# Cross attention with a second attention beside it: two small softmax operations on Pool, the exponential behind the transposed copies, and two products of the keys exchanged

## The chip, the cores and the metric

The kernel runs on one core of one Trainium2 chip. The metric is the device time of one execution in microseconds (us); the time before is 937.95 us, the median of 3 runs (937.41 to 938.43). A core has five engines that run side by side, each with its own queue of instructions: TensorE (PE) for matmuls, VectorE (DVE), ScalarE (ACT) and GpSimd (Pool) for everything elementwise, and SyncE (SP), which here only issues DMAs. An instruction waits at the head of its engine's queue until the instructions it depends on have signalled, and all behind it wait as well.

## What is computed

For 16 batch elements there are 100 query rows of 640 features (x) and 722 context rows of 384 features. The last 4 context rows are tokens of their own. All is float32.

```
query, keyt, valt = x @ Wq, enc @ Wk, enc @ Wv        # enc: 718 context rows
hs = mha(query, keyt, valt)                           # 8 heads of 80
ca_q1 = einsum('btc,th->bch', ca, Wq_ca)[:, indices]  # ca: 4 tokens, 100 picked rows
ca_hs1 = mha(ca_q1, x, x)
ca_q2, ca_k2, ca_v2 = ca_hs1 @ Wq, ca @ Wk_ca, ca @ Wv_ca
out = (hs + mha(ca_q2, ca_k2, ca_v2)) @ Wout + b_out + x
```

The first attention (hs) is large. The other two, called the second attention here, are small; the change is in the softmax of the last of them, which has 100 rows, 8 heads and 4 tokens, so 100 x 32 numbers.

## The kernel before, in words

The batch loop (L1218) makes 16 passes, b = 0 to 15. A pass interleaves three things: the first attention of element b, the keys and values that are needed next (values of b, keys of b+1), and the second attention of b+1 in its first half and of b in its second half. From L1217 on the order is written by hand: every engine's queue holds its instructions in the order in which the program text issues them, and no scheduler moves them.

PE's order in a pass of the usual kind (b = 1 to 14) is: scores of element b (L622, three groups), the product z of the second attention (L810) and y for the next element (L748), then 15 products for the values (L442, class `Values`, called vv) and 15 for the keys (L473, class `Keys`, kk) in turns, then the last chunk of the keys (L567), in some passes an output projection (L1033), in odd passes the queries of the next two elements (L543), and the attention times the values (L1433).

The values and the keys are formed by a scheme with 15 products of sums of input blocks in place of 18 plain ones. Products are accumulated in five PSUM banks, A to E, by the order in `V_PLAN` and `K_PLAN` (L104, L122). Each entry names the bank, the product's form and the place (u, g) of the result to which the bank, as it stands after this product, is added. `Blocks.go` (L404) issues the product, then the drain: a copy on ACT (L415) if the place is new, else an add on DVE (L413). As a bank goes on being accumulated, the next product in the same bank must wait until the bank has been read:

```
for out, left in self.places(at, to):
    if to in self.begun:
        self.moved = nc.vector.tensor_tensor(out, left, out, ALU.add)
    else:
        self.moved = nc.scalar.copy(out, left)
```

The keys' last six entries are, before: B (place 0,1), C (0,1), A (0,1), C (2,1), B (0,0), A (1,1). The first of these is a copy on ACT, the C after it an add on DVE. In a usual pass the end of the product stage issues, by L1346 to L1358: two products vv and one kk; `subtract(0)` and `exponential(0)`; vv; `subtract(1)`; vv; two kk; `exponential(1)`; vv; two kk; then vv and kk in turn, twice. After that come the loads for b+2, `subtract(2)`, `exponential(2)` and the last chunk of the keys. `subtract(i)` (L1240) is a DVE instruction on 120 x 1600 numbers that takes the maximum of the first attention's scores from them in place; both inputs are in SBUF. `exponential(i)` (L1248) is ACT's.

The maximum itself is found by `Maximum` (L658) in steps: transposes and reductions on DVE, then a copy that spreads it (on ACT, L696), then a transpose on DVE (`over`, L704).

The second attention is in the class `Second`. `scores1` (L776) is Pool's: four multiplies (L783) and three adds (L790) of 100 x 800 numbers, for element b+1; the first one waits for the DVE instruction `seen`, the end of the maximum's third part. `scores2` (L837), for element b, forms on DVE the sum s2 (L840), its maximum mx2 (L847), the difference e2 (L849), and on ACT the exponential (L852). `softmax3` (L855) forms on DVE the sum (L858), its reciprocal (L859) and the product p2 (L861). `values2` (L866) is Pool's again: four multiplies by p2 (L875) and three adds (L882), 100 x 640.

The class `Last` ends an element. `turn` and `place` (L932, L937) transpose its result and lay it down with 12 to 20 or so small copies on ACT (L948). `load` (L904) fetches rows of x and adds the bias on Pool (L915, the xn adds). In the passes b = 3, 6, 8, 11 and 13, the pair passes, the projection of two row blocks is done as one (`sums` L1006, `project_pair` L1016): there Pool makes the sum of two blocks (L1014), then, among PE's products, differences (L1050, L1053) and a form of the weights (L1054) that PE multiplies with. After that Pool makes the second attention's keys (L720) and the sums for the next keys and values (L508).

In a usual pass Pool's queue thus holds, before: scores1 of b+1, the xn adds (pair passes), values2 of b, the sums and the projection's operands (pair passes), the vb loads (L832), L720, L508.

Of the kernel before, what the change touches and what calls it, by code (L numbers as in the profile page):

```python
# [9 lines left out]
AF = mybir.ActivationFunctionType  # L10
# [6 lines left out]
CAD, T = 384, 4  # L17
# [28 lines left out]
SCALE = float(D) ** -0.5  # L46
# [72 lines left out]
    ("A", 5, (1, 1)),  # L119
]  # L120

K_PLAN = [V_PLAN[k] for k in (0, 1, 2, 3, 4, 6, 5, 7, 9, 11, 8, 12, 10, 13, 14)]  # L122


A_RAW = {(0, 0): 0, (0, 1): 1, (0, 2): 2, (1, 1): 3, (1, 2): 4, (2, 0): 5, (2, 1): 6}
# [10 lines left out]
def kernel(  # L136
# [18 lines left out]
    nc = tc.nc  # L155
# [220 lines left out]
    def first_values(i, enc, engines, halves=(0, 1), get=psum):  # L376

        u, j = KC[i]
        for g in halves:
            engine = engines[g]  # L380
            v_ps = get(f"v_ps_0_{i}_{g}")
            for c in range(CC):
                nc.tensor.matmul(
                    v_ps[:KN, : H // 2],
                    a_raw(enc, u, c)[:, j * KN : (j + 1) * KN],
                    wv_sb[:, 2 * c + g],
                    start=(c == 0),
                    stop=(c == CC - 1),
                )
            engine(  # L390
                block(i, g)[:, :, :D],
                v_ps[:KN, : H // 2].rearrange("p (h d) -> p h d", d=D),
            )
# [333 lines left out]
    class Second:  # L727
# [45 lines left out]
                ],  # L773
            )

        def scores1(self, behind=None):  # L776
            b, g = self.b, self.g
            e = e1[:S].rearrange("p (h s) -> p h s", h=NH)
            for t in range(T):
                to = e if t == 0 else product_tile(f"e1_{b}_{t}")[:S].rearrange(  # L780
                    "p (h s) -> p h s", h=NH
                )
                first = nc.gpsimd.tensor_tensor(  # L783
                    to,
                    self.ca[:, t, :].unsqueeze(1).to_broadcast([S, NH, S]),
                    g[:, :, t].unsqueeze(2).to_broadcast([S, NH, S]),
                    ALU.mult,
                )
                if t:
                    nc.gpsimd.tensor_tensor(e, e, to, ALU.add)  # L790
                elif behind:
                    wait_for(first, behind)
# [41 lines left out]
            )  # L834
            return vb

        def scores2(self):  # L837
            b, z = self.b, self.z
            s2 = small.tile([S, NH, T], F32, tag="s2", name=f"s2_{b}")
            nc.vector.tensor_reduce(  # L840
                s2.rearrange("p h t -> p (h t)"),
                z.rearrange("p h k -> p k h"),
                AX.X,
                ALU.add,
            )
            mx = small.tile([S, NH], F32, tag="mx2", name=f"mx2_{b}")
            nc.vector.tensor_reduce(mx, s2, AX.X, ALU.max)  # L847
            e = small.tile([S, NH, T], F32, tag="e2", name=f"e2_{b}")
            nc.vector.tensor_tensor(  # L849
                e, s2, mx.unsqueeze(2).to_broadcast([S, NH, T]), ALU.subtract  # L850
            )
            nc.scalar.activation(e, e, AF.Exp, scale=SCALE)  # L852
            self.e = e

        def softmax3(self):  # L855
            b, e = self.b, self.e
            sm = small.tile([S, NH], F32, tag="sm2", name=f"sm2_{b}")
            nc.vector.tensor_reduce(sm, e, AX.X, ALU.add)  # L858
            nc.vector.reciprocal(sm, sm)  # L859
            p2 = small.tile([S, NH, T], F32, tag="p2", name=f"p2_{b}")  # L860
            nc.vector.tensor_tensor(  # L861
                p2, e, sm.unsqueeze(2).to_broadcast([S, NH, T]), ALU.mult
            )
            self.p2 = p2
# [280 lines left out]
    second = Second(0, xT, ca_0)  # L1145
# [72 lines left out]
    for b in range(B):  # L1218
        p = b // 2
        e_in, now = enc, second  # L1220
        enc, second = enc_next, second_next
# [56 lines left out]
        if b == 0:  # L1278
            second.scores1()
            m_next = load_m(b + 2)  # L1280
            kk.go(3)
            top.go(3)
            first_values(3, e_in, (act, act), get=bank)
            top.go(1)
            kk.go(2)
            now.scores2()
            first_values(0, e_in, (act, act), (0,), bank)
            top.go()
            kk.go(3)
            first_values(0, e_in, (act, act), (1,), bank)  # L1290
            now.softmax3()
            kk.go(2)
            subtract(0)
            exponential(0)
            kk.go(2)
            subtract(1)
            kk.go(3)
            exponential(1)
            second_next, enc_next = loads()
            less = subtract(2)  # L1300
            exponential(2)
            last_keys(b + 1, enc)
            enc_next = load_rest(b + 2, enc_next)
            keys(m_next)
            now.values2(less)
            enc_sums(enc_next)
            second.softmax1(4)
        elif b + 1 < B:
            vv = Values(b, e_in)

            def both(n):
                vv.go(n)
                kk.go(n)

            forms = [wout_sb[:, 2 * i : 2 * i + 2, k * (H // 2) : (k + 1) * (H // 2)]
                     for i in range(2) for k in range(2)]
            if b == 2:
                for o, left, right in (
                    (forms[1], forms[1], forms[0]),
                    (wout2[:, 0], forms[3], forms[1]),  # L1320
                    (wout2[:, 1], forms[2], wout2[:, 0]),
                ):
                    nc.gpsimd.tensor_tensor(o, left, right, ALU.subtract)
            elif last.b - 1 in PAIRS:
                nc.gpsimd.tensor_tensor(wout2[:, 0], wout2[:, 0], forms[0], ALU.add)
            second.scores1(seen)
            if b == 1:
                now.load()
            last.load()
            top.go(3)  # L1330
            both(3)
            now.scores2()
            top.go(1)
            if b > 1:
                last.place()
            both(2)
            both(2)
            top.go()
            both(1)
            now.softmax3()  # L1340
            if b == 1:
                nc.gpsimd.tensor_tensor(last.hs[:S], last.hs[:S], last.hs2, ALU.add)
            now.values2()
            if last.b in PAIRS:
                last.sums()
            vv.go(2)  # L1346
            kk.go(1)
            subtract(0)
            exponential(0)
            vv.go(1)  # L1350
            subtract(1)
            vv.go(1)
            kk.go(2)
            exponential(1)
            vv.go(1)
            kk.go(2)
            both(1)
            both(1)  # L1358
            if b == 1:
                for f in list(wv_there):  # L1360
                    nc.scalar.copy(wv_sb[:, W_AT[f]], wv_there.pop(f))
            second.load()
            if b == 1:
                nc.gpsimd.dma_start(out=bias, in_=bout[0].partition_broadcast(P))
            second_next, enc_next = loads()
            if b + 2 < B:
                m_next = load_m(b + 2)
            subtract(2)
            exponential(2)
            last_keys(b + 1, enc)  # L1370
            if b + 2 < B:
                enc_next = load_rest(b + 2, enc_next)
            if b == 1:
                last.transpose()
            if last.b in PAIRS:
                second.softmax1(3)
                last.project_pair()
                if last.b == max(PAIRS):
                    nc.sync.dma_start(
                        out=forms[1],  # L1380
                        in_=wout[: 2 * P, H // 2 :].rearrange("(c p) n -> p c n", p=P),
                    )
            second.softmax1()
        else:
            room = enc_tile("spare").rearrange("p f k -> p (f k)")
            spare.extend(room[:, i * H : (i + 1) * H] for i in range(2))
            last.transpose()
            vv = Values(b, e_in)
            last.load()
            mine.load()  # L1390
            top.go(3)
            vv.go(3)
            last.project_few(len(OC) - 2)
            now.scores2()
            top.go(1)
            vv.go(2)
            top.go()
            vv.go(3)
            now.softmax3()
            now.values2()  # L1400
            vv.go(2)
            subtract(0)
            exponential(0)
            vv.go(5)
            for i in (1, 2):
                subtract(i)
                exponential(i)
            last.project()
# [105 lines left out]
```

## Time and profile before

| what | before |
|---|---|
| median of 3 runs | 937.95 us (937.41 to 938.43) |
| the profiled execution | 936.77 us, span 935.1 us |
| granted TensorE clock | 1.0 of full speed |
| L849 (e2, DVE) | 16 instructions, 900 ns median, 191 to 1249 ns |
| L861 (p2, DVE) | 16 instructions, 193 ns median, 191 to 1573 ns |
| L852 (exponential, ACT) | 16 instructions of 229 ns; ACT idle 27.2 us before them |
| L1240 (subtract, DVE) | 48 instructions, mean 2257 ns, 1810 to 2893 ns |
| L875 (multiply, Pool) | 64 instructions, mean 1882 ns, shortest 1264 ns |
| L720 (Pool, 128 x 64 and 128 x 96) | 70 instructions, median 294 ns |
| Pool idle before L783 for DVE's most | 116.7 us in 9 waits |

The span goes from the first to the last instruction; the rest of an execution's time lies around it. A row of the timeline gives the start in us from the span's start, the time, the engine, the source line and what is written from what; "xN" means N instructions in the row, and a bracket says how long the engine stood idle before it and who released it. PE has two rows: matmuls (PE) and the weight loads (PEld) that run ahead of them. The ends of matmuls are modelled, so their starts are the better measure.

### The profile page before, as it was taken

What the parts mean: (1) busy time and instruction counts of PE and PEld (TensorE: products, weight loads), DVE (VectorE), ACT (ScalarE), POOL (GpSimd) and SP (SyncE); (2) the same over time, 40 slices, a digit from 0 to 9 for tenths busy, and PEclk for the clock granted to TensorE, in tenths of its full rate; (3) what the DMA queues carried; (4) which work ended last, traced back from release to release, by engine and by line L of the source; (5) the groups of instructions that cost most, each with busy time, mean ns of one, the idle gap of its engine ahead of it and who ended that gap; (6) DMA issues with size and microseconds to landing.
All of it is one profiled execution on the core that took longest, in us unless ns stands there. A gap on an engine that the chain in (4) does not pass through costs nothing.

```text
span 935.1 us, 25893 instructions
## 1 busy us (share of the span) xinstructions
PE 926.5 (99%) x11130; PEld 786.6 (84%) x11130; DVE 699.4 (75%) x1111; ACT 434.6 (46%) x836; POOL 674.8 (72%) x615
## 2 busy tenths in 40 slices
PE   9999999999999999999999999999999999999998
PEld 6998989797797979888798787988879888797866
DVE  3859794989739796795957869589883898838884
ACT  2235443736337363562726536264651737417341
POOL 5657998788937877496884968658895588946723
PEclk9999999999999999999999999999999999999999
DMA  8732022040300304031030400205030050310201
GB/s 258 260 96 70 24 78 64 12 143 2 107 26 23 104 11 122 2 103 53 26 106 3 124 31 30 74 2 153 3 102 31 2 153 2 102 45 2 81 19 40
DMA packets 49673, 62.82 MB, mean 67 GB/s; under 512 B 14072, under 2 KB 38200, under 8 KB 49560
## 3 DMA queue, kind: packets, MB, share of 16 engines
q1 hardware_dynamic: 45512, 51.49, 18.3%
q0 software_dynamic: 3024, 8.53, 3.0%
q8 instruction: 87, 1.43, 0.6%
q10 hardware_dynamic: 1024, 1.15, 0.4%
q14 instruction: 26, 0.21, 0.1%
HBM read 55.59 MB, written 5.57 MB: 65 GB/s over the span
## 4 chain that ended last, share of the span: by engine, by line
PE 86%; DVE 11%; issue 1%; DMA 1%; ACT 1%; POOL 0%; DVEq 0%
PE a_ps L1433 12%; PE s_ps L622 12%; PE v_psA L442 8%; PE kT_ps L567 8%; PE q_ps L543 7%; PE v_psB L442 7%; PE k_psA L473 6%; PE o_ps L1033 5%; PE k_psB L473 5%; PE v_psC L442 3%; DVE st L1240 3%; DVE vs L413 2%; PE k_psC L473 2%; DVE kT L413 2%; DVE most L1252 2%; PE y_ps L748 2%
## 5 line engine op out<-in xcount | busy, mean ns | idle before, releaser
L783 POOL TENSOR_TENSOR e<-ca,g 100x800 f32<-100x800 f32 x64 | 99.5, 1564 | 130.6 <-DVE most L1252 116.7
L875 POOL TENSOR_TENSOR hs<-vb,p 100x640 f32<-100x640 f32 x64 | 119.8, 1882 | 49.7 <-DVE p L861 24.1
L508 POOL TENSOR_TENSOR enc<-enc 128x240 f32<-128x240 f32 x135 | 106.2, 796 | 20.4 <-DMA enc<-in_enct 13.3
L1433 PEld LDWEIGHTS a_ps<-vs,st 120*36 120x36 f32 (+3 forms) x3072 | 109.2, 125 | 4.9 <-issue 4.8
L1433 PE MATMUL a_ps<-vs,st 120*36 120x81 f32 (+3 forms) x3072 | 112.0, 233 | 0.0
L442 PE MATMUL v_psA<-wv_sb,enc 128*120 128x320 f32 x352 | 109.6, 434 | 0.0
L1240 DVE TENSOR_TENSOR st<-st,over 120x1600 f32<-120x1600 f32 x48 | 108.3, 2257 | 0.0
L882 POOL TENSOR_TENSOR hs<-hs,hs 100x640 f32<-100x640 f32 x48 | 99.1, 2065 | 3.8
L622 PE MATMUL s_ps<-qp,kT 32*120 32x100 f32 x3072 | 98.3, 263 | 0.0
L622 PEld LDWEIGHTS s_ps<-qp,kT 32*120 32x120 f32 x3072 | 95.5, 179 | 1.7 <-issue 0.2
L639 ACT COPY st<-s_ps 120x800 f32<-120x800 f32 x64 | 49.7, 829 | 100.6 <-PE s_ps L622 100.6
L790 POOL TENSOR_TENSOR e<-e,e 100x800 f32<-100x800 f32 x48 | 92.3, 1922 | 3.8
L442 PE MATMUL v_psB<-wv_sb,enc 128*120 128x320 f32 x296 | 91.8, 433 | 0.0
L1248 ACT ACTIVATE st<-st 120x1600 f32<-120x1600 f32 x48 | 73.8, 1538 | 32.6 <-DVE st L1240 32.4
L473 PE MATMUL k_psA<-enc,wk_sb 128*128 128x240 f32 x360 | 87.6, 366 | 0.0
L1252 DVE TENSOR_TENSOR most<-most,st 120x800 f32<-120x800 f32 x64 | 68.4, 1068 | 22.4 <-ACT st L633 21.3
L473 PEld LDWEIGHTS k_psA<-enc,wk_sb 128*128 128x128 f32 x360 | 68.3, 190 | 16.7
L442 PEld LDWEIGHTS v_psA<-wv_sb,enc 128*120 128x120 f32 x352 | 63.2, 183 | 22.6 <-issue 0.5
L473 PE MATMUL k_psB<-enc,wk_sb 128*128 128x240 f32 x300 | 73.1, 366 | 0.1
L442 PEld LDWEIGHTS v_psB<-wv_sb,enc 128*120 128x120 f32 x296 | 54.1, 183 | 21.9 <-DVE vs L413 0.4
L1445 DVE RECIPROCAL rs<-a_ps 100x4 f32<-100x4 f32 x32 | 5.8, 181 | 85.6 <-PE a_ps L1433 85.6
L948 ACT COPY hsT<-turned_hs 32x160 f32<-32x160 f32 (+7 forms) x244 | 67.7, 278 | 3.0
(167 smaller groups left out, 1852.8 us busy)
## 6 DMA issues: line engine op xcount, KB each, us to landing
vb<-va_d POOLq DMA_DIRECT2D x32, 250.0 KB, 3.6
vb<-va_d SPq DMA_DIRECT2D x32, 250.0 KB
enc<-in_enct SPq DMA_DIRECT2D x30, 240.0 KB
enc<-in_enct SPq DMA_DIRECT2D x15, 360.0 KB
xT<-in_xt SPq DMA_DIRECT2D x8, 500.0 KB
rest<-in_enct SPq DMA_DIRECT2D x31, 120.0 KB
xn<-in_x SPq DMA_DIRECT2D x11, 320.0 KB
out<-xn SPq DMA_DIRECT2D x11, 320.0 KB
```

What stands on the lines that cost most here:

```text
L442: nc.tensor.matmul(at[0][j][:KN, : H // 2], a_form(self.enc, f)[:, j * KN : (j + 1) * KN], wv_there.get(f, wv_sb[:, W_AT[f]]), start=first ...
L473: nc.tensor.matmul(at[:, i * KT : (i + 1) * KT], wk_sb[:, W_AT[f], i], a_form(self.enc, f), start=(first and i == 0), stop=last, skip_grou ...
L508: nc.gpsimd.tensor_tensor(out, left, right, op)
L567: nc.tensor.matmul(bank[:, i * KT : (i + 1) * KT], weights[c], a_raw(enc, u, c), start=(i == 0 and c == 0), stop=(c == CC - 1), skip_group ...
L622: nc.tensor.matmul(s_ps[r][:n, 256 * a + lo : 256 * a + hi], kT[rows, c, u, j * KN : (j + 1) * KN], rhs, start=(a == 0 and c == 0), stop=( ...
L783: first = nc.gpsimd.tensor_tensor(to, self.ca[:, t, :].unsqueeze(1).to_broadcast([S, NH, S]), g[:, :, t].unsqueeze(2).to_broadcast([S, NH, ...
L790: nc.gpsimd.tensor_tensor(e, e, to, ALU.add)
L875: first = nc.gpsimd.tensor_tensor(to, self.vb[t][:S].rearrange("p (h d) -> p h d", h=NH), p2[:, :, t].unsqueeze(2).to_broadcast([S, NH, D] ...
L882: nc.gpsimd.tensor_tensor(sums, sums, to, ALU.add)
L1240: return nc.vector.tensor_tensor(st[i], st[i], top.over[:KN].unsqueeze(1).to_broadcast([KN, 2, ROWS]), ALU.subtract,)
L1252: most_now = nc.vector.tensor_tensor(most[:KN], most[:KN], st[i][:, u], ALU.max)
L1433: nc.tensor.matmul(a_v[lo:hi, h % 4], st[i // 2][: KEYS[i], i % 2, h * S + lo : h * S + hi], block(i, h // 4)[: KEYS[i], h % 4], start=(i ...
```

## The change

In `K_PLAN` the entries C (2,1) and B (0,0) near the end change places, so that the keys' last five products are C, A, B, C, A.

`scores1` can be issued in parts. In the usual passes (b = 1 to 14) Pool gets three of the four multiplies with their two adds, then the difference e2 of `scores2` (with an engine as its argument, here Pool), then the fourth multiply with its add. The exponential is a method of its own and is issued behind the spread copies and behind `place`. In the last pass e2 is on Pool as well, its exponential stays where it was; in the first pass e2 stays on DVE. The product p2 of `softmax3` goes to Pool in all passes, directly ahead of the multiplies of `values2` in the usual ones, and ahead of L720 in pass 0. The numbers computed are the same.

```diff
-K_PLAN = [V_PLAN[k] for k in (0, 1, 2, 3, 4, 6, 5, 7, 9, 11, 8, 12, 10, 13, 14)]
+K_PLAN = [V_PLAN[k] for k in (0, 1, 2, 3, 4, 6, 5, 7, 9, 11, 8, 12, 13, 10, 14)]
...
-        def scores1(self, behind=None):
+        def scores1(self, behind=None, tokens=range(T)):
...
-            for t in range(T):
+            for t in tokens:
...
-        def scores2(self):
+        def scores2(self, engine=nc.vector):
...
-            nc.vector.tensor_tensor(
+            engine.tensor_tensor(
                 e, s2, mx.unsqueeze(2).to_broadcast([S, NH, T]), ALU.subtract
             )
-            nc.scalar.activation(e, e, AF.Exp, scale=SCALE)
             self.e = e
+
+        def exponentials2(self):
+            nc.scalar.activation(self.e, self.e, AF.Exp, scale=SCALE)
...
-            nc.vector.tensor_tensor(
+            nc.gpsimd.tensor_tensor(
                 p2, e, sm.unsqueeze(2).to_broadcast([S, NH, T]), ALU.mult
             )
...
-            second.scores1(seen)
+            second.scores1(seen, range(T - 1))
+            top.go(3)
+            both(3)
+            now.scores2(nc.gpsimd)
+            second.scores1(None, range(T - 1, T))
             if b == 1:
                 now.load()
             last.load()
-            top.go(3)
-            both(3)
-            now.scores2()
             top.go(1)
             if b > 1:
                 last.place()
+            now.exponentials2()
             both(2)
...
-            now.scores2()
+            now.scores2(nc.gpsimd)
+            now.exponentials2()
```

More of the change, by code (lines that the diff above doesn't have):

```diff
@@ L1393 @@
             last.project_few(len(OC) - 2)
-            now.scores2()
+            now.scores2(nc.gpsimd)
+            now.exponentials2()
             top.go(1)
```

## The prediction

> **What bounds the kernel now.** I read the page first, then who waits for whom, then the chain of waits, then the timeline of single passes. A pass is one round of the batch loop, numbered by b.
>
> ```profile
> PE 926.5 (99%) x11130; PEld 786.6 (84%) x11130; DVE 699.4 (75%) x1111; ACT 434.6 (46%) x836; POOL 674.8 (72%) x615
> ```
>
> TensorE (PE) is busy for 926.5 of 935.1 us, so work taken off another engine pays only where PE stands still for it. The list of waits has one PE wait that returns in every pass:
>
> ```profile
> PEld k_psC L473 <- DVE kT L413: 7.8, 15, 1.0
> PE k_psC L473 <- DVE kT L413: 1.9, 4, 0.6
> ```
>
> The keys' second C product waits until VectorE (DVE) has added the first one out of the same bank. Part of the weight load's wait is covered by the matmul before it, so I take the loss from PE's starts. From the start of the eleventh keys' A product to the product after C there should be two keys' products of 0.81 us, 1.62 us. The time above that is, for passes 0 to 14: 0.59, 0.17, 0.33, 0.91, 0.33, 0.33, 0.17, 0.33, 0.15, 0.33, 0.33, 0.75, 0.34, 0.75, 0.36. The sum is 6.17 us. Pass 7 shows the cause:
>
> ```profile
> 463.33 2.85 DVE L1240 TENSOR_TENSOR st<-st,over 120x1600 f32<-120x1600 f32 x1
> ...
> 464.80 0.56 ACT L415 COPY kT<-k_psB 128x480 f32<-128x480 f32 x1 [0.84 <-PE k_psB L473]
> ...
> 466.10 0.81 DVE L413 TENSOR_TENSOR vs<-v_psB,vs 120x640 f32<-120x640 f32 x1
> ...
> 466.83 0.64 DVE L413 TENSOR_TENSOR kT<-k_psC,kT 128x480 f32<-128x480 f32 x1
> ...
> 467.53 0.70 PEld L473 LDWEIGHTS k_psC<-enc,wk_sb 128*128 128x128 f32 x4 [0.44 <-DVE kT L413]
> 467.53 1.08 PE L473 MATMUL k_psC<-enc,wk_sb 128*128 128x240 f32 x4
> ```
>
> DVE's second subtraction, two adds, then PE. The subtraction takes 2.85 us here and 1.81 us at its shortest: it waits for a multiply of Pool (L875) in flight. Bank B, in contrast, was emptied by ScalarE (ACT) at 465.36, 2 us before PE gets there.
>
> **Second bound: the five pair passes** (3, 6, 8, 11, 13), where Pool makes operands for PE's output projection. In pass 6:
>
> ```profile
> 402.38 1.26 DVE L861 TENSOR_TENSOR p<-e,sm 100x32 f32<-100x32 f32 x1
> 403.56 1.81 DVE L1240 TENSOR_TENSOR st<-st,over 120x1600 f32<-120x1600 f32 x1
> 403.77 5.55 POOL L875 TENSOR_TENSOR hs<-vb,p 100x640 f32<-100x640 f32 x2 [0.19 <-issue]
> ...
> 419.12 0.73 POOL L1014 TENSOR_TENSOR hsT<-sum,hsT 128x256 f32<-128x256 f32 x1
> ...
> 420.56 2.32 PE L1033 MATMUL o_ps<-wout,hsT 128*128 128x320 f32 x8
> ...
> 421.95 0.73 POOL L1053 TENSOR_TENSOR hsT<-hsT 128x256 f32<-128x256 f32 x1 [0.30 <-PE o_ps L1033]
> ...
> 422.63 1.54 POOL L1054 TENSOR_TENSOR wout<-wout,wout_sb 128x640 f32<-128x640 f32 x1
> ...
> 424.23 0.84 PEld L1033 LDWEIGHTS o_ps<-wout,hsT 128*128 128x128 f32 x4 [0.24 <-POOL wout L1054]
> ```
>
> Two multiplies of 1.27 us take 5.55 us: DVE's subtractions shut Pool out twice. From the end of the xn adds (403.58) to the projection Pool has no hole. L1054 ends at 424.17 and PE's load follows at 424.23, its matmul at 424.33, just when the four matmuls before it are done. So there PE has no reserve against Pool; at the L1014 sum it has 0.58 us (matmul at 420.56; earliest 0.15 after the sum's end at 419.85).
>
> **The change part by part.**
>
> *The exchange.* B comes at the place of C, and C two products later (keys' B 0.81, values' B 1.08). B needs only ACT's copy, 2 us early. C's drain, due at 467.48 in pass 7, is wanted at 469.2: 1.7 us to spare, 1.2 us in pass 3 (worst stall). The values' B product needs the add at 466.10 only, 0.6 us ahead of C's drain and wanted 0.8 later. The DVE queue behind keeps its number of adds. The third subtraction follows at the same distance; its exponential ends at 475.23, and the attention matmuls read that part not before 2.3 us into their stage. Even in short passes (pass 4: exponential ends 311.98, stage starts 312.71) that leaves 3 us. Gain: 6.17 us if nothing else holds PE; 3.44 us of it in passes without a pair, 2.73 us in pair passes.
>
> *Subtraction of the maximum (L849), DVE to Pool, passes 1 to 15.* DVE loses 0.91 us (0.19 of work, the rest waiting for Pool's add). It stands in a stretch where DVE catches up anyway (idle 0.28 us before the values' A add at 455.37), so nothing reaches PE: 0. On Pool nothing of this shape is in the trace. From 128x64 (0.29 us, L720) and 128x256 (0.73 us) a line gives 0.21 for 32 elements; from above 0.35 (L720's 128x96 mean). I take 0.25, near the smaller row. Pool has a 0.08 us hole at this place, which it fills: 0.17 us on Pool. It needs DVE's maximum, ready at 392.53 in pass 6 while Pool arrives at 397.0: no wait. Behind it: the fourth product and its add, the vb loads' issue in pass 1, the xn adds. SP's queue keeps its order.
>
> *Exponential behind the copies.* ACT no longer stands 27.2 us in all for L849; the spread copies and the transposed copies (place) start some 1.3 us earlier. The exponential comes when they end, in pass 6 about 399.7, and Pool's result is there at 397.3. Its reader, DVE's sum at 401.94, is bound by adds. Behind it ACT's C copies wait for PE until 401.6. Result: 0. In pass 1, without copies, it waits for Pool until about 123.7, just ahead of the C copies at 123.79: 0 to 0.2 us, not on PE's path.
>
> *The product with 1/sum (L861), DVE to Pool, all passes.* DVE saves 0.1 us, 1.2 to 1.5 in pair passes, where it waited for an xn add. Subtraction 0 then takes the port itself, before or after the second xn add; with the exchange PE does not feel it. On Pool: 0.25 plus 0.08 until the dependent multiply starts, 0.33. Pool loses the same three rounds to the subtractions, of some 1.6 us; the first cost only 1.56, as it began with xn's end: 0.05 more.
>
> *Pool's delay.* 0.17 + 0.33 + 0.05 = 0.55 us each pass, bounds 0.4 and 0.87. In other passes a hole takes it (2.39 us before L720 in pass 2, 8.87 us before L783 in pass 7). In pair passes it reaches PE. L1053 no longer waits for PE (0.27 us: in pass 3 it could start at 249.97 and starts at 250.24), so L1054 and the matmul behind it come 0.55 - 0.27 = 0.28 us later than before, and whatever PE saved at C is waited away here. Five times: +1.4 us (0.65 to 3.0).
>
> Sum: -3.44 + 1.4 = **-2.0 us** (-2.8 to -0.4). The profiled execution took 936.77 us (span 935.1) and would take 934.8; against the median of 937.95 us that is **936.0 us**. The tail (pass 15) has a Pool hole of 24.11 us and changes by 0.1 either way.
>
> The Trainium skill speaks against the move twice. "SBUF — State Buffer", Who interferes with whom, says that a DVE instruction with two SBUF inputs and a Pool instruction that reads SBUF exclude each other for whole instructions; the 2.85 and 5.55 us rows agree. By that rule every instruction more on Pool is one more that may have to stand behind a subtraction. "GPSIMD Engine Reference", section 3.1, has Pool's tensor_tensor at 1.96 times DVE's time. By it L849 and L861 would take 0.37 us each, an estimate, Pool's delay would be 0.79, and the sum -0.8 us.
>
> **Rivals.**
>
> *Pair passes not held up (0.25).* If Pool's two instructions fall into gaps that I do not see, the pair passes end neutral (-3.4) up to the full gain (-6.2): 934.5 down to 931.8 us, 933.4 in the middle. For it: in pass 6 DVE takes the port between Pool instructions at other moments once L861 is gone. Against: three rounds remain three rounds.
>
> *Pool loses one more port round in each pair pass (0.12): slower.* L861 stands alone between xn and L875 and gives DVE one more gap to enter. A round is 1.6 us: delay 2.15, 1.88 per pair pass, 9.4 less 3.44: +6.0, 944 us. It decides from a delay of 1.34 us on (5 x 1.07 - 3.44 = +1.9). For it: L915, L875 and L882 each show such doubled times. Against: DVE has only three such subtractions there.
>
> *The exchange does nothing (0.08).* If PE waited at B or at the values' B for DVE just as long, only the pair cost would stay, +1.4 (0.65 to 3.0): 939.3 us. Against: the ACT row at 464.80.
>
> **How the numbers follow.** The forecast has 0.55, its own range 935.2 to 937.6. About 0.2%, 1.9 us, is what a measurement of this kernel can tell from no change. Somewhat over half of the forecast lies below -1.9 us (0.29); with the first rival 0.54 faster. The rest of the forecast and most of the third rival are the same, 0.31; the second and a part of the third slower, 0.15. The range goes from the first rival's lower half to the third's price, 932.8 to 939.3, and leaves out about 0.17.
>
> **What would show it.** Right: no wait of k_psC for DVE kT; PE's step from the keys' A to the values' B 1.62 us plus one B product and no hole; L849 and L861 on POOL at 0.2 to 0.35 us; waits of o_ps for POOL grown in the five pair passes, L1014 among them; L1240's mean below 2.26 us. Wrong: new PE waits outside pair passes, Pool instructions of 0.5 us and more, or pair passes shorter than before.

## The result

| | before | after |
|---|---|---|
| median of the runs | 937.26 us (936.42 to 938.44, 12 runs) | 935.30 us (933.59 to 936.92, 12 runs) |
| the profiled execution | 936.77 us, span 935.1 us | 933.59 us, span 931.9 us |

The ratio is 0.9978, 95% interval 0.9969 to 0.9987: 2.0 us faster. The profiled execution of after is the fastest of its 12, so its 3.2 us are more than the median shows. In the changed kernel L861 is L863, L875 is L877, L882 is L884, L1014 is L1016, L1033 is L1035, L1053 and L1054 are L1055 and L1056, L1240 is L1242, L1433 is L1439.

The page of after, busy times and the engines' shares of the chain that ended last:

```profile
PE 925.3 (99%) x11130; PEld 787.9 (85%) x11130; DVE 684.8 (73%) x1080; ACT 433.7 (47%) x836; POOL 684.1 (73%) x646
...
PE 95%; POOL 4%; DMA 1%; issue 0%; DVE 0%; ACTq 0%; ACT 0%; POOLq 0%
```

DVE has given 31 instructions to Pool, and its share of the chain, 11% before, is gone. The waits of the weight loads in after (us in total, times, longest):

```profile
PEld o_ps L1035 <- POOL wout L1056: 2.5, 5, 0.6
...
PEld o_ps L1035 <- POOL hsT L1016: 1.7, 3, 0.8
```

The wait of k_psC (7.8 us before) is missing. In its place PE waits for Pool: for L1056 5 times as before, but 2.5 us where it was 1.2, and newly for the sum, L1016. Pass 7 of after, the place of the removed wait:

```profile
461.24 2.89 DVE L1242 TENSOR_TENSOR st<-st,over 120x1600 f32<-120x1600 f32 x1
...
464.78 0.64 DVE L413 TENSOR_TENSOR kT<-k_psC,kT 128x480 f32<-128x480 f32 x1
465.01 0.80 PEld L473 LDWEIGHTS k_psB<-enc,wk_sb 128*128 128x128 f32 x4
465.21 0.97 PE L473 MATMUL k_psB<-enc,wk_sb 128*128 128x240 f32 x4
...
467.10 0.97 PE L473 MATMUL k_psC<-enc,wk_sb 128*128 128x240 f32 x4
```

The subtraction is as long as before and bank C's drain as late (it ends at 465.42), but PE goes on with B and comes back to C at 467.10. The products from the values' first A to the keys' transposes take 28.32 us in every pass from 1 to 14 (before 28.48 to 29.23), 5.6 us less in all, and pass 0, from its first z product to its attention stage, is 0.65 us shorter. Of the 0.65 us 0.05 belong to an earlier wait of pass 0, at a product in bank B that follows an add of DVE: 0.40 us before, 0.35 after, and 0.35 to 0.69 in the other profiles.

Pass 6 of after on Pool, and PE's load for the pair's last operand:

```profile
400.14 3.08 DVE L1242 TENSOR_TENSOR st<-st,over 120x1600 f32<-120x1600 f32 x1
401.49 1.83 POOL L863 TENSOR_TENSOR p<-e,sm 100x32 f32<-100x32 f32 x1
403.39 4.08 POOL L877 TENSOR_TENSOR hs<-vb,p 100x640 f32<-100x640 f32 x2
...
417.27 0.73 POOL L1016 TENSOR_TENSOR hsT<-sum,hsT 128x256 f32<-128x256 f32 x1
417.94 1.10 POOL L832 DMA_DIRECT2D vb<-va_d  x2
419.05 0.74 POOL L1052 TENSOR_TENSOR hsT<-hsT,hsT 128x256 f32<-128x256 f32 x1
419.86 0.72 POOL L1055 TENSOR_TENSOR hsT<-hsT 128x256 f32<-128x256 f32 x1
420.54 1.54 POOL L1056 TENSOR_TENSOR wout<-wout,wout_sb 128x640 f32<-128x640 f32 x1
...
422.13 0.84 PEld L1035 LDWEIGHTS o_ps<-wout,hsT 128*128 128x128 f32 x4 [0.44 <-POOL wout L1056]
```

p2 (L863) now stands through a round of DVE's subtraction that a multiply stood through before: some 0.24 of its 1.83 us are work, since it took 0.234 us in pass 13, where it came ahead of the subtraction, and the two multiplies after it need 4.08 us instead of 5.55. L1055 has lost its idle bracket (0.30 before): Pool is late, and PE waits 0.44 us for L1056 (0.24 before).

How long the pair's product takes (the stage from the first o_ps matmul to PE's next stage) can be told from one number in every profile of this study: when Pool ends L1054. That is 6.30 us after the first o_ps matmul at the earliest, where Pool itself waits for PE ahead of L1053, and later where Pool's queue is late. In pass 3, measured from the first o_ps matmul:

| kernel | end of the sums L1014 | end of L1054 | stage |
|---|---|---|---|
| before | 1.97 us | 6.31 us | 9.70 us |
| after | 3.09 us | 7.18 us | 10.56 us |
| after, again (e3) | 3.42 us | 7.52 us | 10.90 us |
| the exchange alone (e1) | 2.90 us | 6.99 us | 10.38 us |
| exponential moved, nothing on Pool (e7) | 2.42 us | 6.52 us | 9.91 us |

The stage is L1054's end and 3.39 us more in every row, and so it is in passes 3, 11 and 13 of all 13 profiles; in passes 6 and 8 it is 3.48 us more. In the kernel before PE was so late, through its wait at C, that it met Pool exactly.

### The profile page after: what moved, and what is told of

It reads as the page before. It is cut to its first block, busy times and chain, and to the rows that moved or that the text cites. A ratio compares the mean times of both kernels' runs of the same rounds, so it can differ in the third digit from the quotient of the medians.

```text
span 931.9 us, 25889 instructions
## 1 busy us (share of the span) xinstructions
PE 925.3 (99%) x11130; PEld 787.9 (85%) x11130; DVE 684.8 (73%) x1080; ACT 433.7 (47%) x836; POOL 684.1 (73%) x646
## 4 chain that ended last, share of the span: by engine, by line
PE 95%; POOL 4%; DMA 1%; issue 0%; DVE 0%; ACTq 0%; ACT 0%; POOLq 0%
PE s_ps L622 13%; PE a_ps L1439 12%; PE v_psA L442 10%; PE v_psB L442 8%; PE kT_ps L567 7%; PE k_psA L473 7%; PE q_ps L543 7%; PE k_psB L473 6%; PE o_ps L1035 5%; PE v_psC L442 3%; PE k_psC L473 2%; PE v_ps L383 2%; PE y_ps L748 2%; PE v_psD L442 2%; PE v_psE L442 2%; PE k_psE L473 1%
## 5 line engine op out<-in xcount | busy, mean ns | idle before, releaser
L783 POOL TENSOR_TENSOR e<-ca,g 100x800 f32<-100x800 f32 x64 | 99.2, 1561 | 126.5 <-DVE most L1254 116.0
L508 POOL TENSOR_TENSOR enc<-enc 128x240 f32<-128x240 f32 x135 | 105.1, 788 | 16.7 <-DMA enc<-in_enct 9.6
L1242 DVE TENSOR_TENSOR st<-st,over 120x1600 f32<-120x1600 f32 x48 | 115.2, 2402 | 0.0
L1439 PEld LDWEIGHTS a_ps<-vs,st 120*36 120x36 f32 (+3 forms) x3072 | 109.3, 125 | 5.2 <-issue 5.0
L1439 PE MATMUL a_ps<-vs,st 120*36 120x81 f32 (+3 forms) x3072 | 112.3, 233 | 0.1
L884 POOL TENSOR_TENSOR hs<-hs,hs 100x640 f32<-100x640 f32 x48 | 103.7, 2160 | 3.8
L877 POOL TENSOR_TENSOR hs<-vb,p 100x640 f32<-100x640 f32 x64 | 91.9, 1446 | 9.0 <-issue 4.7
L543 PE MATMUL q_ps<-xT,wq_sb 128*128 128x200 f32 x400 | 69.1, 333 | 0.0
```

Of the source, the lines that this page charges most:

```text
L508: nc.gpsimd.tensor_tensor(out, left, right, op)
L543: nc.tensor.matmul(q_ps[:, : 2 * S].rearrange("p (j s) -> p j s", j=2), wq_sb[:, c, n * P : (n + 1) * P], xT[:, :, c, :], start=(c == 0), ...
L783: first = nc.gpsimd.tensor_tensor(to, self.ca[:, t, :].unsqueeze(1).to_broadcast([S, NH, S]), g[:, :, t].unsqueeze(2).to_broadcast([S, NH, ...
L877: first = nc.gpsimd.tensor_tensor(to, self.vb[t][:S].rearrange("p (h d) -> p h d", h=NH), p2[:, :, t].unsqueeze(2).to_broadcast([S, NH, D] ...
L884: nc.gpsimd.tensor_tensor(sums, sums, to, ALU.add)
L1242: return nc.vector.tensor_tensor(st[i], st[i], top.over[:KN].unsqueeze(1).to_broadcast([KN, 2, ROWS]), ALU.subtract,)
```

## The experiments

The kernel before is the base of the ratios; the runs of before that they are measured against had medians of 937.8 us (e1 to e4), 937.57 us (e5 to e8) and 937.58 us (e9 to e11). A sum of the pair stages is that of passes 3, 6, 8, 11 and 13; it is 48.67 us before and 50.98 us after. The label e2 stands at the head of the second experiment; in the text e2 is the difference of `scores2`, and p2 the product of `softmax3`.

**e1, the exchange alone.** The only edit to before is the one in the plan:

```diff
-K_PLAN = [V_PLAN[k] for k in (0, 1, 2, 3, 4, 6, 5, 7, 9, 11, 8, 12, 10, 13, 14)]
+K_PLAN = [V_PLAN[k] for k in (0, 1, 2, 3, 4, 6, 5, 7, 9, 11, 8, 12, 13, 10, 14)]
```

> Only the exchange of the last C and B products; all of the second softmax stays on DVE and ACT as before. Theory (the exchange takes away PE's wait, Pool's added work takes part of it back in the pair passes): no wait of k_psC for DVE in any pass, the values' and keys' stage at 28.32 us in all usual passes; Pool's sums and L1054 come no later than before, so the pair passes gain up to 0.27 us each (the reserve of L1053), together 1.1 us, the others 3.44 us: 4.5 us faster than before, that is faster than the whole change. Rival (the exchange is worth just what the whole change brought): 2.0 us faster. Rival (Pool's part makes the gain): 0.

Measured: 933.44 us (5 runs), ratio 0.9954 (0.9942 to 0.9967), -4.3 us. The product stages are at 28.32 us (28.41 in pass 11), the pair stages sum to 50.38 us. The waits of the weight loads:

```profile
PEld o_ps L1033 <- POOL wout L1054: 2.1, 5, 0.6
...
PEld o_ps L1033 <- POOL hsT L1014: 1.5, 3, 0.7
```

PE waits for Pool although Pool has not one instruction more: it comes to the pair's product earlier, and Pool does not. And the exchange alone is twice as good as the whole change; the rest of the change costs 2 us.

**e2, the moves to Pool alone.** After, with the plan of before:

```diff
-K_PLAN = [V_PLAN[k] for k in (0, 1, 2, 3, 4, 6, 5, 7, 9, 11, 8, 12, 13, 10, 14)]
+K_PLAN = [V_PLAN[k] for k in (0, 1, 2, 3, 4, 6, 5, 7, 9, 11, 8, 12, 10, 13, 14)]
```

> Everything of the change but the exchange: the keys' last products in the old order. Theory: the wait of k_psC for DVE kT is back, in passes without a pair within 0.1 us of before (the second subtraction ends at the same place, 24.4 us after z); in the pair passes what is won at C is waited for again at Pool's sums. Time against before: -0.5 us (-1.5 to +1.5). Rival (Pool's part makes the gain): -2 us.

Measured: 939.33 us (11 runs), ratio 1.0013 (1.0004 to 1.0022), +1.2 us. The waits of the weight loads:

```profile
PEld k_psC L473 <- DVE kT L413: 5.9, 12, 0.7
...
PEld o_ps L1035 <- POOL hsT L1016: 3.1, 3, 1.2
PEld o_ps L1035 <- POOL wout L1056: 2.2, 5, 0.6
```

The wait at C is gone in passes 3, 11 and 13 (product stages of 28.32 us), and there PE runs into Pool: pair stages of 10.57, 10.88 and 11.02 us. In passes 6 and 8 PE still stands at C, comes 0.3 us later than before, and finds Pool done (9.79 and 9.78 us). The trace shows why DVE came in time in just those three. Its first subtraction starts 18.24 us after the first z product in all five pair passes, since DVE no longer has p2 ahead of it. In passes 3, 11 and 13 Pool is later, and the subtraction gets in ahead of the second bias addition and ends at 20.4 to 20.7 us; in passes 6 and 8 it stands behind that addition until 21.4. The second one ends at 23.5 to 23.8 us there, at 24.5 here, and the drain of C follows. Whether the two parts of the change add up the times don't show: -4.3 and +1.2 give -3.1, measured -2.0, and the three intervals leave room for both.

**e3, the changed kernel once more,** without an edit.

> The changed kernel once more, for a second profile and for the spread of its runs (933.6 to 936.9 us so far). Theory: the stages up to the projection are the same to 0.02 us as in the first profile, 28.32 us for the values and keys; what differs between runs is time that PE loses without a wait in the attention and scores stages (6.91 and 7.28 us when undisturbed), as in pass 12 of the first profile. Rival: it differs in the pair passes, by who gets there first, Pool or DVE. Time against before: -2 us by both.

Measured: 935.76 us (7 runs), ratio 0.9977 (0.9966 to 0.9987). Its profiled execution took 936.22 us, span 934.5 us, 2.6 us more than that of the first profile. Of this the pair stages have 1.31 us (they sum to 52.29 us), the attention and score stages of passes 4 and 12 some 0.6 us, the work ahead of the first z product 0.59 us, pass 0 0.12 us.

**e4, Pool freed ahead of the sums.** On after: both bias additions behind the sums, the loads of the next values' rows behind the pair's product.

```diff
-                    nc.gpsimd.tensor_tensor(to, to, bias[at : at + n, cols], ALU.add)
...
                 last.sums()
+                last.add_bias()
...
-            second.load()
+            if last.b not in PAIRS:
+                second.load()
...
                 last.project_pair()
+                second.load()
...
```

> The changed kernel with Pool's queue shortened ahead of the projection's sums in the five pair passes: the xn adds are issued behind the sums, the vb loads behind the project_pair. Nothing else moves. Theory (in pair passes Pool's lateness eats what the exchange gives): o_ps no longer waits for Pool, the projection's stage is 9.70 us or less, five passes together 2.4 us shorter than in the changed kernel: 4.4 us faster than before. Rival (the pair passes are held by something else, or DVE now waits for the late xn adds): as the changed kernel, -2 us.

Measured: 935.68 us (9 runs), ratio 0.9976 (0.9966 to 0.9986): nothing gained, pair stages 52.16 us. Pool in pass 3, and PE's load:

```profile
245.01 0.73 POOL L1022 TENSOR_TENSOR hsT<-sum,hsT 128x256 f32<-128x256 f32 x1
245.70 3.04 POOL L923 TENSOR_TENSOR xn<-xn,bias 128x640 f32<-128x640 f32 x2
248.69 0.73 POOL L1058 TENSOR_TENSOR hsT<-hsT,hsT 128x256 f32<-128x256 f32 x1
...
250.18 1.54 POOL L1062 TENSOR_TENSOR wout<-wout,wout_sb 128x640 f32<-128x640 f32 x1
...
251.78 0.84 PEld L1041 LDWEIGHTS o_ps<-wout,hsT 128*128 128x128 f32 x4 [0.43 <-POOL wout L1062]
```

The sums end 1.03 us after the first o_ps matmul (3.09 in after), but the two additions, 3.0 us, now stand between them and L1062, which ends at 7.01: stage 10.40. DVE did wait for the additions, as the rival said (5.3 us in all), and handed it to PE (3.8 us). Yet the stage is L1062's end and 3.39 us here too, and from the sums to L1062 Pool's queue has no idle time, so it is the later deadline that decided.

**e5, of the Pool moves p2 alone,** with the exchange:

```diff
...
-            nc.vector.tensor_tensor(
+            nc.gpsimd.tensor_tensor(
                 p2, e, sm.unsqueeze(2).to_broadcast([S, NH, T]), ALU.mult
```

> The exchange, and of the moves to Pool the probabilities' multiplication p2 alone; e2 stays on VectorE and its exponential where it was. The exchange alone gave 0.9954 (-4.3 us), the whole change 0.9977 (-2.1): 2.2 us are given back by the moves. Theory (each operation put on Pool delays the sums of the pair passes by its own time: in pass 6 p2 took 0.21 us of the 0.27 by which Pool was later, e2 0.06): p2 gives back most of the 2.2 us, 5 x 0.21 = 1.1 us at least, -2.5 to -3.3 us, ratio 0.9965 to 0.9973. Rival (the place of the exponential behind the copies, not Pool's work, makes Pool late): p2 gives back 0.3 us or less, ratio 0.9954 to 0.9958.

Measured: 935.45 us (7 runs), ratio 0.9973 (0.9963 to 0.9984), -2.5 us; pair stages 51.51 us.

**e6, e2 alone,** that is, after with p2 back on DVE:

```diff
-            nc.gpsimd.tensor_tensor(
+            nc.vector.tensor_tensor(
                 p2, e, sm.unsqueeze(2).to_broadcast([S, NH, T]), ALU.mult
```

> The exchange, with e2 on Pool ahead of the scores' last product, its exponential behind the transposed copies, and p2 left on VectorE: the whole change without p2's move. Theory: e2 costs Pool 0.06 us net, so 5 x 0.06 = 0.3 us are given back, -4.0 us, ratio 0.9957 (0.9952 to 0.9962). Rival: it holds most of the cost, -2.1 to -2.8 us, ratio 0.997 to 0.9977.

Measured: 934.85 us (9 runs), ratio 0.9968 (0.9958 to 0.9978), -3.0 us by the ratio; pair stages 51.18 us. The middle lies between the theory and the rival, and the interval reaches into both: the time alone does not tell them apart.

**e7, the exponential alone behind the copies,** with the exchange, nothing on Pool:

```diff
...
-            nc.scalar.activation(e, e, AF.Exp, scale=SCALE)
...
             if b > 1:
                 last.place()
+            now.exponentials2()
...
```

> The exchange, with the exponential of the second softmax behind the transposed copies and nothing on Pool. Theory: ScalarE's order alone gives nothing back, -4.3 us, ratio 0.9954 (0.9949 to 0.9959). Rival: an exponential that comes later makes the sum, the reciprocal, p2 and with them Pool's four multiplications and sums later in the pair passes: 1 to 2 us given back, ratio 0.9965 to 0.9977.

Measured: 932.89 us (5 runs), ratio 0.9954 (0.9942 to 0.9967): the exchange's own number, so ScalarE's order costs nothing that this measurement could see (its interval is 1.2 us to either side). The pair stages sum to 49.79 us.

These three and e1 give Pool's delay directly. From Pool's first multiply of a pass (L783) to the end of the sums it takes, in the five pair passes, 31.39 to 31.42 us in before, 31.41 to 31.45 in e1 and 31.40 to 31.43 in e7: the same each time. With e2 on Pool it is 31.49 to 31.86 (0.20 us more on average), with p2 31.61 to 32.06 (0.32), with both 31.69 to 31.89 (0.35; 0.38 in e3, 0.41 with the old plan). This is what the moves cost. In passes 3, 11 and 13 it goes to PE whole, in 6 and 8 in part, where Pool begins early enough to keep some reserve. By their medians e5 lies 2.0 us over e1 and e6 2.0 us over e7; 5 x 0.32 = 1.6 and 5 x 0.20 = 1.0 us are within what their intervals leave open.

What differs from run to run is when Pool begins. In passes 6 and 8 it begins 4.41 or 4.42 us after the first z product, in nearly every profile; in passes 3, 11 and 13 it begins 4.48 to 5.35 us after it. Pool and DVE ahead of pass 3 in e1 (its first z product is at 212.16):

```profile
211.65 2.77 DVE L1252 TENSOR_TENSOR most<-most,st 120x800 f32<-120x800 f32 x2 [1.47 <-ACT st L633]
...
215.08 2.01 DVE L1252 TENSOR_TENSOR most<-most,st 120x800 f32<-120x800 f32 x2
...
217.32 3.04 POOL L783 TENSOR_TENSOR e<-ca,g 100x800 f32<-100x800 f32 x2 [3.75 <-PE v_psD L442]
```

and ahead of pass 6 in e1 (383.36):

```profile
382.86 2.02 DVE L1252 TENSOR_TENSOR most<-most,st 120x800 f32<-120x800 f32 x2 [1.48 <-ACT st L633]
...
385.59 2.01 DVE L1252 TENSOR_TENSOR most<-most,st 120x800 f32<-120x800 f32 x2
...
387.83 3.04 POOL L783 TENSOR_TENSOR e<-ca,g 100x800 f32<-100x800 f32 x2 [12.37 <-DVE most L1252]
```

In pass 3 Pool's additions of encoder rows (L508) run beside DVE's first two maxima, which take 2.77 us instead of 2.02; DVE then ends later the last two, which Pool's first multiply needs. The bracket in pass 3 names PE, but Pool starts 0.23 us after the end of the last maximum in all five pair passes of all 13 profiles. In passes 6 and 8 the L508 rows end over 6 us ahead of the first two maxima, which take 2.02 us every time; in passes 3, 11 and 13 they take 2.40 to 2.96 us, and Pool starts 2.9 us after the second of them every time. So how the L508 rows fall against the maxima decides the start there, and with it up to 0.9 us per pass. No run moved these rows on purpose.

**e8, a version meant to be better.** The exchange alone, the second row's bias addition behind the sums, the loads behind the pair's product:

```diff
...
                     nc.sync.dma_start(out=to, in_=rows[:, cols])
-                    nc.gpsimd.tensor_tensor(to, to, bias[at : at + n, cols], ALU.add)
+                    if r - 1 != PAIRS.get(self.b):
+                        self.add_bias(r, to, at, n, cols)
...
                 last.sums()
+                r = PAIRS[last.b] + 1
+                n = OC[r][1]
+                for at, cols in last.parts(n):
+                    last.add_bias(r, last.xn[r][at : at + n, : cols.stop - cols.start], at, n, cols)
...
-            second.load()
+            if last.b not in PAIRS:
+                second.load()
...
                 last.project_pair()
+                second.load()
```

> A version meant to be the better one: the exchange alone, and in the pair passes the second of the two rows' bias additions is issued on Pool behind the sums of the pair, not ahead of them, and the loads of the values' rows for the next second attention behind the pair's product; all else as before. Theory (in the pair passes PE waits for Pool's queue): Pool's sums end some 1.5 us earlier, the difference of the weights ends ahead of PE, the output stage of the five pair passes falls to 9.70 us from the 9.77 to 10.46 of the exchange alone, some 1.9 us in all: -6.2 us against the kernel before, ratio 0.9934. Rival (as when both additions stood behind the sums: VectorE then waits for the later addition and hands the wait on to PE): nothing gained, ratio 0.9952 to 0.9975, with a wait of PE or VectorE for the second row in the pair passes.

Measured: 931.85 us (5 runs), ratio 0.9944 (0.9931 to 0.9956), -5.3 us by the ratio, less than the theory's -6.2, which the interval reaches; pair stages 48.62 us, as the theory had them. Pool in pass 3 (the first o_ps matmul is at 244.66), and PE's load:

```profile
244.98 0.73 POOL L1018 TENSOR_TENSOR hsT<-sum,hsT 128x256 f32<-128x256 f32 x1
245.66 1.54 POOL L919 TENSOR_TENSOR xn<-xn,bias 128x640 f32<-128x640 f32 x1
247.16 0.73 POOL L1054 TENSOR_TENSOR hsT<-hsT,hsT 128x256 f32<-128x256 f32 x1
248.75 0.73 POOL L1057 TENSOR_TENSOR hsT<-hsT 128x256 f32<-128x256 f32 x1 [0.85 <-PE o_ps L1037]
249.43 1.54 POOL L1058 TENSOR_TENSOR wout<-wout,wout_sb 128x640 f32<-128x640 f32 x1
250.91 1.10 POOL L832 DMA_DIRECT2D vb<-va_d  x2
...
251.02 0.84 PEld L1037 LDWEIGHTS o_ps<-wout,hsT 128*128 128x128 f32 x4 [0.24 <-POOL wout L1058]
```

The bracket of L1057 is back: Pool waits 0.85 us for PE. No wait of PE for the sums is left, and that for L1058 is 1.2 us in all, as in the kernel before.

**e9, the whole change in e8's order.** The same diff as e8's, on after.

> The whole change, with the order that gave 0.9944 (-5.7 us) on the exchange alone: in the pair passes the second row's bias addition on Pool behind the sums, the loads of the next values' rows behind the pair's product. Theory (the moves to Pool cost nothing by themselves but for the pair passes, where PE waits for Pool's queue; this order takes some 1.5 us out of that queue ahead of the sums, more than the 0.3 us that the moves add): the moves cost nothing any more, -5.7 us, ratio 0.9944 (0.9939 to 0.995), output stages of the pair passes at 9.70 to 9.80 us. Rival (the moves cost elsewhere too, through longer subtractions on VectorE or PE's losses without a wait): 2 us are given back here as well, -3.5 us, ratio 0.996 to 0.9967.

Measured: 932.23 us (5 runs), ratio 0.9940 (0.9927 to 0.9952), -5.6 us by the ratio. Its pair stages sum to 48.63 us. Once Pool has room in the pair passes, its two new instructions cost nothing; and they bring nothing either, for e8 without them is as fast.

**e10, only the addition moved,** e8 without its last two edits.

> The exchange alone, with only the second row's bias addition moved behind the sums; the loads of the values' rows stay where they were, ahead of the pair's product. Theory (the addition of 1.54 us ahead of the sums is what PE waits for): all or nearly all of e8's gain, -5.2 to -5.7 us, ratio 0.9944 to 0.995. Rival (the loads' issue of 2 x 1.1 us on Pool ahead of the weights' difference is the wait): the addition behind the sums only moves the 1.54 us from ahead of the sums to ahead of the difference, and PE's wait for the difference grows: -3.5 to -4.3 us, ratio 0.9954 to 0.9963.

Measured: 934.56 us (6 runs), ratio 0.9970 (0.9958 to 0.9982), -2.8 us by the ratio; pair stages 51.20 us. Pool in pass 3:

```profile
245.36 0.73 POOL L1018 TENSOR_TENSOR hsT<-sum,hsT 128x256 f32<-128x256 f32 x1
246.05 1.54 POOL L919 TENSOR_TENSOR xn<-xn,bias 128x640 f32<-128x640 f32 x1
247.53 1.10 POOL L832 DMA_DIRECT2D vb<-va_d  x2
248.64 0.74 POOL L1054 TENSOR_TENSOR hsT<-hsT,hsT 128x256 f32<-128x256 f32 x1
...
251.72 0.84 PEld L1037 LDWEIGHTS o_ps<-wout,hsT 128*128 128x128 f32 x4 [0.83 <-POOL wout L1058]
```

The rival's mechanism: 1.5 us taken from ahead of the sums is put ahead of the difference, and PE waits 0.83 us there. The middle is even worse than the rival's -3.5 to -4.3 us, and the interval reaches into that range; the pair stages are 0.8 us longer than in e1.

**e11, only the loads moved,** the last two edits of e8 alone, on the exchange.

> The exchange alone, with only the loads of the values' rows moved behind the pair's product; both bias additions stay ahead of the sums. Theory (the sums' end decides, and it does not move): -4.3 to -4.6 us, ratio 0.9951 to 0.9954, PE's wait for the sums as in the exchange alone and its wait for the weights' difference down from 0.6 us at most to 0.2. Rival (the loads' issue is the wait): -5.7 us, ratio 0.9944, output stages of the pair passes at 9.70.

Measured: 932.91 us (5 runs), ratio 0.9949 (0.9938 to 0.9961), -4.8 us by the ratio; pair stages 49.47 us. The waits of the weight loads:

```profile
PEld o_ps L1033 <- POOL hsT L1014: 1.5, 3, 0.6
PEld o_ps L1033 <- POOL wout L1054: 1.2, 5, 0.2
```

As the theory had it: the wait for the sums stays, the one for the difference falls to 1.2 us. By their intervals e8, e9 and e11 can't be told apart, nor e1 from any of them. By the pair stages of one profile each the loads alone gain 0.9 us over e1, the addition alone loses 0.8, and both together gain 1.8: two deadlines, and the addition helps at the first only if the loads make room at the second.

## Why the prediction was right in its sum, and where not

- **The wait at C, -6.17 us: right.** Measured -5.6 in passes 1 to 14, where the stall list was right pass by pass, and -0.65 in pass 0, where 0.59 was taken. Without the change of pass 0's earlier wait it is 0.60, and in the other profiles with the exchange 0.58 to 0.60. The rival that the exchange does nothing is refuted.
- **The part outside the pair passes, -3.44 us: right.** Of the 5.6 us, 2.73 lie in pair passes; the other 2.87 and pass 0's 0.65 make 3.5.
- **Pair passes held by Pool: right as a mechanism.** e1 and the L1016 wait show it, so the rival that they are not held up is refuted (the middle of its two prices is 933.1, not 933.4 us); and in e8, where Pool is in time, the pair stages are back at 9.69 to 9.78 us. The reserve of 0.27 us was right too: in before the sums end at 1.97, and 4.08 us of queue behind them make 6.05 against 6.31.
- **Pool's delay, 0.55 us: the size was off.** It is 0.35 and 0.38 us, under the lower bound of 0.4. (The upper bound of 0.87 does not follow from the row named for it: 0.35 us for each instruction makes 0.75.) The instructions' own time was priced rightly (L849 takes 0.238 us, L863 0.234 in the one pass where it came ahead of DVE; 0.25 was taken). Alone, e2 has 0.20 us where 0.17 was taken and p2 0.32 where 0.33 was, on average over the five pair passes. In passes 6 and 8 the two add up (0.08 and 0.21 alone, 0.28 together, 0.31 in e3); the averages of each alone are raised by single passes (0.43 and 0.64 us in pass 11), and why these stand out was not followed. The extra 0.05 for one more round did not show.
- **Pair passes +1.4 us: mis-sized.** Against before the five pair passes changed by -0.4 us in the first profile and by +0.9 in the second; that they came out shorter in the first was named as a sign of being wrong. Two steps failed: the delay of 0.55 us was too large, and Pool's start was taken as fixed, where in passes 3, 11 and 13 it moves by up to 0.9 us from run to run.
- **What the sum had no term for.** PE lost more in the attention and score stages of passes 4 and 12 (+0.6 us in the first profile of after, +1.2 in the second), and the first z product came 0.1 and 0.7 us later. For the first profile -3.5 - 0.4 + 0.6 + 0.1 gives -3.2 us, its span's change; for the second -3.4 + 0.9 + 1.2 + 0.7 gives -0.6, its span's change. So the forecast's -2.0 us is met by the median, with 1.2 us too much for the pair passes on average and about as much missing elsewhere. That these cancel is luck: nothing shows that the losses elsewhere belong to the change. Over the 13 profiles those stages of passes 4 and 12 lose 0.3 to 2.0 us against undisturbed ones (0.3 in e7 and 1.8 in e1, neither with anything new on Pool), and the first z product comes at 67.0 to 68.9 us, earliest in the one profile of before.
- **The rival of one more round lost by Pool in each pair pass: refuted.** In pass 6 the three rounds are p2's 1.83, the first pair of multiplies' 4.08 and a later one's 2.74 us, as many as before.
- **L861 on Pool at 0.2 to 0.35 us: wrong as a sign.** L863 took over 0.5 us in 15 of its 16 passes (median 1.64 us), which the prediction named as a sign of being wrong. The delay stayed small all the same, because the multiplies behind it got shorter: their mean fell from 1882 to 1446 ns.
- **L1240's mean below 2.26 us: wrong.** It is 2402 ns (2257 before; 2331 in e1, 2394 in e5). Of the 7.0 us more in all, 3.8 lie in the first subtraction, which now starts earlier and itself waits for the bias addition that p2 waited for, 3.08 us in pass 6. That wait was moved and not removed. Another 2.6 us lie in the third subtraction, which is longer with the exchange alone too (4.4 us in e1). None of this shows as a wait of PE: after the exchange PE does not look for DVE there.
- **Of the two rules of the Trainium skill.** L849 on Pool takes 0.238 us and at its shortest on DVE 0.191 us, 1.25 times as long; "GPSIMD Engine Reference", section 3.1, has 1.96 times, for an add of 2048 elements; for the 32 elements a row here that is too much. p2's 1.83 us behind a subtraction agree with "SBUF — State Buffer", Who interferes with whom.

## What to carry to other kernels

Before taking a wait off the busiest engine, measure how much later each other engine could be at the next meeting point: here it was 0.27 us, and 1.7 us of the 2.7 us gained in the pair passes were waited away again (e1). Work added to that engine then costs time too: with e2 or p2 on it Pool came 0.2 or 0.3 us later in each pair pass, and of the exchange's 4.3 us 2.0 were left. When one engine feeds another at two points, list the queue ahead of each deadline: moving work from ahead of the first to ahead of the second helps only if the second has room. Operations moved off an engine that is not waited for gain nothing, as e8 against e9 shows.

## What was not expected of the hardware

PE loses time in the attention stage of passes 4 and 12 with no releaser in the profile, at a granted clock of 1.00. The undisturbed stage takes 6.91 us; in the various profiles it took 6.91 to 8.38 us in pass 12 and 6.91 to 7.90 in pass 4, and the score stage behind it, 7.27 us where undisturbed, up to 7.84. In e1 it shows as PE's own wait:

```profile
PE a_ps L1433 <- issue: 1.2, 1, 1.2
```

In both passes this stage follows the keys directly while the loads for a later batch run. That alone is not it: passes 2 and 10 have the same order of stages, and in after a DMA share of 0.78 and 0.70 in the stage's first 7 us, without a loss; pass 12 has 0.71 with one. No experiment here was aimed at it, and the cause stays open.
